# One decoder layer with a mixture of experts on one core: the first slot's turn moved up, and VectorE's last stages moved behind `down`

## The chip, the core and the metric

The kernel runs on one core of a Trainium2 chip. A core has TensorE (PE in the profile, with its weight loads as PEld), VectorE (DVE), ScalarE (ACT), GpSimd (POOL) and SyncE (SP, which here only issues DMAs). Each engine works through its own instructions in the order in which the program issues them, and waits for other engines through semaphores. The metric is the time of one execution on the device in microseconds (us); the profile's span is the stretch inside it from the first to the last recorded event. All times below are of the kernel before.

## The reference: what is computed

The input x has 16 sequences of 128 tokens and 256 channels. Three residual layers follow one another, each on a layer norm of x:

```python
x = x + attn(layernorm(x))       # latent attention: 16 heads, 72 latents, causal
x = x + birwkv(layernorm(x), ctx)
x = x + ffn(layernorm(x))        # 8 experts of 512, two of them for each token

# attn
kv = xn @ latent_w + latent_b;  q[h] = xn @ Wd_w[h] + Wd_b[h]
y[h] = softmax(causal(q[h] @ kv.T / 4)) @ kv;   out = concat(y) @ out_w + out_b
# birwkv: sums over the past and over the future that decay by exp(w) a step, ek = exp(ctx)
wkv = (Af + Ab + exp(u + ctx) * ctx) / (Bf + Bb + exp(u + ctx))
out = sigmoid(xn) * wkv
# ffn: top 2 of 8 by logits, each gate a softmax with far logits masked out
out = sum over the two experts e of gate_e * (silu(xn @ wg[e].T) * (xn @ wu[e].T)) @ wd[e].T
```

All of it is float32.

## The kernel before

**Steps.** The program is one loop over steps s. Steps 0 to 63 are the attention's units: unit s is sequence b = s // 4 and head group s % 4 (four heads each). A unit's scores are computed in step s, its softmax is normalized (`normalize`) in step s + 1, and its probabilities are turned (`turn_probs`: four PE transposes and a copy `aT` by ScalarE) and multiplied with the values in step s + 2. So steps 64 and 65 still hold the end of the attention.

From step 64 on each step also has an expert slot, j = s − 64. A slot is 128 tokens that go to one expert. The loop has 36 of them in its order; three more, which are rarely used, stand behind a condition after slot 27. For slot j:

- `fetch(j)` gathers the 128 rows into `xr` by an indirect DMA that GpSimd issues. It is called three slots ahead.
- `bring(j)` copies the expert's gate weights (ScalarE) and up weights (VectorE) into the buffers `w`. Called one slot ahead.
- `turn(j)` transposes `xr` on PE into the PSUM tile `pxr` and copies that to `xT` (VectorE, L930). Called one slot ahead.
- `up(j)` is two products of 16 matmul records each in the profile: gate product `pg`, then up product `pu` (PE, L966), then `sl` = silu(pg) (ScalarE, L976) and `hT` = sl · pu (VectorE, L978).
- `down(j)` multiplies with the third weight (PE, `pd`, L988), scales by the gate into `y` (VectorE, L999) and adds `y` into the rows of `acc` by an indirect DMA of GpSimd (L1004). Called one slot later: step s holds `up(j)` and then `down(j − 1)`.

**The order inside a step.** Everything else is put into steps by hand. `at(step, place, fn, ...)` notes a piece of work under a step and a place, and `run(s, place)` calls the pieces of that place in the order in which they were noted. As the engines keep the order of issue, the place decides what a piece stands behind on each engine. A slot step of the kernel before issues:

1. `scores` (steps up to 63), `normalize`, place "pre", `turn_probs`, place "A", the maxima and exponentials of the scores (up to 63), place "B", the values' product and its copy out (up to 65);
2. in step 64 only: the attention's pools are closed, the pool `hp` for the slots' tiles is opened, then `bring(0)` and `turn(0)`;
3. `fetch(j + 3)`, `bring(j + 1)`, `up(j)`;
4. place "C";
5. `turn(j + 1)`, `down(j − 1)`.

**What stands in the places around the change.** Each sequence b goes through named stages after its attention; tables (`usual`, `last_but_one` for sequence 14, `last` for sequence 15) give each stage a step, counted from 4b, and a place. In order: `project` (PE, L506, the output projection from the tiles `yP`; the last of nine tiles comes back through DRAM, `rest_values`, L500), `residual` (VectorE: sum and statistics; GpSimd: the reciprocal root `rs_b`, L294), `receptance` (VectorE: two small operations into `nr`, L567, which wait for `rs_b`), `receptance_exp` (ScalarE, exp), `wkv_turn` (PE, `pw`, L584), `mix_1` and `mix_2` (VectorE: L588, a reciprocal L593 and a product L594; then a sum on GpSimd, L595), `mix_stats` (VectorE statistics, GpSimd `rs_c`), `store_sum` (SyncE: the sum to `acc`, L598), `mix_shift` (VectorE: `nb_c`, L314), `mix_row` (ScalarE: the normed row, L611), `store_row` (SyncE, L617), `logits_turn` (PE: two transposes `px`, L626), `logits_turned` (VectorE: copy `x2T`, L631), `logits` (PE: `pl`, L638), `logits_out` (VectorE: `src`, L650).

After every four sequences `route(r)` picks the two experts of 512 tokens. It is a generator; each call does the next part: part 1 and 2 the largest and the second largest logit (VectorE), part 3 the selection and masked gates (VectorE, then an exp on ScalarE), part 4 a running count over tokens on PE (`pf`, L691 to L694) and the gates' sum, part 5 each token's place in the experts' lists and the new totals `taken` (VectorE, L712 to L723). Eight further parts scatter entries into `lists` (GpSimd, L727).

Slots are made from tables: after sequences 7, 11 and 15 a generator (`first_table`, `last_table`) reads the totals through a PE product (`counts`, `pc`, L744) and works out, in some 20 small VectorE operations cut into parts, which expert and which stretch of its list each slot has. `list_slots` then loads the lists' entries (`en`, SyncE, L849).

**PSUM.** Tiles are named by a tag; tag "t" has two buffers that `pt`, `pxr`, `pw` and `px` take in the order of issue, so the third such tile waits until the first has been read. Tag "y" has one buffer for the values' product and, in the first slots, `pu`.

Of the kernel before, what the change touches and what calls it, by code (L numbers as in the profile page):

```python
# [19 lines left out]
B = 16  # L20
T = 128
N = B * T
C = 256
# [49 lines left out]
SLOT0 = NU  # L73
# [6 lines left out]
def decoder_kernel(  # L80
# [30 lines left out]
    st = ctx.enter_context(ExitStack())  # L111
# [316 lines left out]
    def scores(b, hg):  # L428
        g, i = divmod(b, GB)
        ps = bank("s", f"ps_{b}_{hg}").rearrange("p (j t) -> p j t", j=HG)  # L430
        nc.tensor.matmul(ps, identb, maskb, start=True, stop=False)
        for j in range(HG):
            nc.tensor.matmul(  # L433
                ps[:, j, :],
                q[g, hg][0:L, j, ts(i, T)],
                kvT[g][:, ts(i, T)],
                start=False,
                stop=(j == HG - 1),
            )
        pss[b, hg] = ps  # L440
# [466 lines left out]
    hpools, xTs, hTs, regs, useds, brought = [], {}, {}, {}, [], {}  # L907
    experts = {mybir.EngineType.Activation: {}, mybir.EngineType.DVE: {}}

    def bring(j):  # L910


        t, k = slots[j]
        to = []
        for n, (engine, copy) in enumerate(zip(experts, (nc.scalar.copy, nc.vector.tensor_copy))):
            into = experts[engine]
            if k % 4 == 0 or j in RARE:
                load_values(t, "ex", j, k, engine, E - 1, into)
            w = hpools[0].tile([P, WU0], F32, tag=f"w{n}", name=f"w{n}_{j}")
            copy(w, wall[:, bass.ds(into.pop(j), 1), n * WU0 : (n + 1) * WU0].rearrange("p o w -> p (o w)"))  # L920
            to.append(w)
        brought[j] = to

    def turn(j):
        xr = xrs.pop(j)
        pt = bank("t", f"pxr_{j}")
        for c in range(NC):
            nc.tensor.transpose(pt[:, ts(c, P)], xr[:, ts(c, P)], ident)  # L928
        xT = hpools[0].tile([P, NC, P], F32, tag="xT", name=f"xT_{j}")
        nc.vector.tensor_copy(xT, pt[:, : NC * P].rearrange("p (c t) -> p c t", c=NC))  # L930
        xTs[j] = xT
# [49 lines left out]
    def down(j):  # L981
        e = regs.pop(j)
        hT = hTs.pop(j)
        pd = bank("mm", f"pd_{j}")

        def products():
            for f in range(NF):
                nc.tensor.matmul(  # L988
                    pd[:, :C],
                    hT[:, f, :],  # L990
                    wall[:, bass.ds(e, 1), WD0 + f * C : WD0 + (f + 1) * C],
                    start=(f == 0),
                    stop=(f == NF - 1),
                )

        products()
        en = entries.pop(j)
        y = hpools[0].tile([P, C], F32, tag="y", name=f"y_{j}", bufs=3)
        nc.vector.tensor_scalar_mul(y, pd[:, :C], en[:, 2:3].bitcast(F32))  # L999
        if j == SF + S2:  # L1000
            nc.sync.dma_start(out2, acc[0:N, :])

        def add():
            nc.gpsimd.indirect_dma_start(  # L1004
                out=acc if j < SF + S2 else out2,
                out_offset=bass.IndirectOffsetOnAxis(ap=en[:, 1:2], axis=0),
                in_=y,
                in_offset=None,
                compute_op=ALU.add,
            )  # L1010

        add()
# [4 lines left out]
    def at(step, place, fn, *args):  # L1017
        plan.setdefault((step, place), []).append((fn, args))

    def run(step, place):  # L1020
        for fn, args in plan.pop((step, place), []):
            fn(*args)
# [6 lines left out]
    for g in range(1, NG):  # L1029
# [43 lines left out]
    }  # L1073
    last = {
        "residual": (7, "B"),
        "receptance": (7, "C"),
        "receptance_exp": (8, "A"),
        "wkv_turn": (8, "B"),
        "mix_1": (8, "C"),
        "mix_2": (8, "C"),  # L1080
        "mix_stats": (9, "B"),
        "store_sum": (9, "C"),
        "mix_shift": (9, "C"),
        "mix_row": (10, "A"),
        "logits_turn": (10, "B"),
        "logits_turned": (10, "C"),
        "store_row": (10, "C"),
        "logits": (11, "B"),
        "logits_out": (11, "C"),
    }  # L1090
    last_but_one = dict(usual)

# [11 lines left out]
    for name in ("wkv_turn", "mix_1", "mix_2"):  # L1104
        last_but_one[name] = (9, "B")
    for name in ("logits_turn", "logits_turned"):
        last_but_one[name] = (11, "B")
    stages = {
        "residual": residual,
        "receptance": receptance,  # L1110
# [14 lines left out]
    for b in range(B):  # L1125
        s = NHG * b
        if b + 1 < B:
            at(s + 2, "pre", load_ctx, b + 1)
        at(s + 1, "C", wkv_exps, b)
        at(s + 2, "B", wkv_back, b)  # L1130
        at(s + 3, "A", wkv_back_add, b)
        at(s + 4, "B", wkv_forth, b)
        at(s + 5, "A", wkv_forth_add, b)
        at(s + 5, "B", project, b, (0, 1))
        at(s + 6, "B", project, b, (2, 3))
        at(s + 6, "C", rest_values, b)
        at(s + 7, "B", project, b, (4, 5))
        at(s + 7, "C" if b < B - 1 else "B", project, b, (6, 7, NP))
        for name, (step, place) in {B - 2: last_but_one, B - 1: last}.get(b, usual).items():
            at(s + step, place, stages[name], b)  # L1140
        if b < E:
            for k in range(3):
                at(s + 11 + k, "C", load_expert, b, k)
        if b % RB == RB - 1:
            r = b // RB
            parts = ((13, "B"), (13, "C"), (14, "B"), (15, "B"), (15, "C"))
            if b == B - 1:
                parts = ((12, "B"), (12, "C"), (13, "B"), (14, "B"), (14, "C"))
            for step, place in parts:
                at(s + step, place, route_part, r)  # L1150
            for k in range(2 * RB):
                if b < B - 1:
                    at(s + 16 + k, "A", route_part, r)
                else:
                    at(s + 15 + k // 4, "AC"[k // 2 % 2], route_part, r)
        if b + 1 in FIRST_B:
            i = FIRST_B.index(b + 1)
            for k in range(6):
                at(s + 18 + k, "C", table_part, i, first_table, i)
            for k in range(0, S1[i], 2):  # L1160
                at(s + 24 + k // 2, "C", list_slots, min(2, S1[i] - k))
        if b == B - 1:
            for k in range(7):
                at(s + 15 + k // 3, "ABC"[k % 3], table_part, "2", last_table)
            for k in range(0, S2, 4):
                at(s + 17 + k // 4, "C", list_slots, min(4, S2 - k))
            for k in range(4):
                at(s + 20 + k, "B", table_part, "3", very_last)
            for k in range(0, S3, 4):
                at(s + 24 + k // 4, "C", list_slots, min(4, S3 - k))  # L1170
# [41 lines left out]
    for s in range(SLOT0 + len(ORDER) + 1):  # L1212
        j = s - SLOT0
        unit = divmod(s, NHG)
        past = divmod(s - 2, NHG)
        if s < NU:
            scores(*unit)
        if 1 <= s < NU + 1:
            normalize(*divmod(s - 1, NHG))
        run(s, "pre")  # L1220
        if 2 <= s < NU + 2:
            turn_probs(*past)
        run(s, "A")
        if s < NU:
            maxima(*unit)
            exps(*unit)
        g, i = divmod(s, UG)
        tiles = [(0, t) for t in late_tiles.get(s, [])]
        if g + 1 < NG:
            tiles += [(g + 1, t) for t in (TILES_1 if g == 0 else TILES)[i]]  # L1230
        made = [(n, t, *query_tile(n, t)) for n, t in tiles[:2]]
        run(s, "B")
        if 2 <= s < NU + 2:
            values(*past)
            values_out(*past)
        for n, t, pq, to in made:
            query_tile_out(n, t, pq, to)
        for n, t in tiles[2:]:
            query_tile_out(n, t, *query_tile(n, t))
        for n, t in tiles:  # L1240
            if t == NP:
                rest_queries(n)
            if t == 5 and n:
                odd_queries(n, 0)
            if t == 7:
                odd_queries(n, 1)
        if j == 0:

            st.close()
            hpools.append(ctx.enter_context(tc.tile_pool(name="hp", bufs=2)))  # L1250
            bring(0)
            turn(0)
        if j >= 0:
            ahead(j + AHEAD, fetch)
            ahead(j + 1, bring)
            ahead(j, up)
        run(s, "C")
        if j >= 0:
            ahead(j + 1, turn)
            if j >= 1:  # L1260
                down(ORDER[j - 1])
        if j == SF + S2 - SKIP:
            for r in RARE:
                if_used(r, whole_slot)
# [55 lines left out]
```

## Time and profile before

| | us |
|---|---|
| median of 3 runs (567.83, 571.44, 572.62) | 571.44 |
| profiled execution | 571.29 |
| its span | 569.6 |
| PE busy | 523.7 (92%) |
| VectorE busy | 326.8 (57%) |
| ScalarE busy | 293.7 (52%) |
| GpSimd busy | 326.6 (57%) |
| `up(0)` starts (step 64) | 336.09 |
| `up(13)` starts (step 77) | 424.52 |
| last `down` starts | 551.72 |

The span's first 320 us are attention, the stretch from 330 to 424 holds the slots beside the last sequences, routing and tables, and from 424 on there are slots alone. In a timeline row the first two numbers are the start and the duration in us, then engine, line and operation, the tile written and the tiles read, and in brackets how long the engine stood idle before and what released it. In a list of waits the three numbers are the sum in us, how often, and the longest.

### The profile page before, as it was taken

The page shows a single profiled execution, that of the slowest core. Times are in us where ns is not written, and L with a number is a line of the kernel's source. Part 1 is how long each engine was busy: PE and PEld are TensorE (multiplying, and loading weights), DVE is VectorE, ACT ScalarE, POOL GpSimd, SP SyncE. Part 2 cuts the span into 40 slices and gives each one's busy share as a digit, 9 for nine tenths or more (in the row PEclk, how much of TensorE's full clock was granted, in tenths as well). Part 3 has the DMA queues.
Part 4 walks back from the last instruction along what each step waited for, and adds up shares of the span by engine and source line. Part 5 has one row for each costly group of instructions (what it writes and reads, how often), then busy time and mean ns, then how long its engine had stood idle before and what let it go on. Part 6 is the DMA issues. An engine that isn't in the chain of part 4 may idle for free. (4 is left out here: it accounts for less than half of the span.)

```text
span 569.6 us, 10246 instructions
## 1 busy us (share of the span) xinstructions
PE 523.7 (92%) x3317; PEld 447.1 (78%) x3334; DVE 326.8 (57%) x831; ACT 293.7 (52%) x891; POOL 326.6 (57%) x379
## 2 busy tenths in 40 slices
PE   4989999999999999999998959989999999998990
PEld 3767788877877877878876648879989999998990
DVE  3435576577886678878668745555563543433330
ACT  1667776786676777767774744332322323222300
POOL 5355656574787665688636873544486545451532
PEclk9999999999999999999997979999999999999996
DMA  4422145364455544121221111233223333235321
GB/s 144 116 66 74 56 139 181 100 184 126 131 146 152 153 137 150 58 76 40 66 66 44 36 48 30 53 56 57 39 30 50 58 57 47 48 51 171 51 36 18
DMA packets 39662, 47.59 MB, mean 84 GB/s; under 512 B 14136, under 2 KB 31416, under 8 KB 39576
## 3 DMA queue, kind: packets, MB, share of 16 engines
q1 hardware_dynamic: 30106, 37.20, 22.3%
q0 software_dynamic: 7936, 9.51, 10.7%
q8 instruction: 28, 0.46, 0.4%
q10 hardware_dynamic: 1566, 0.21, 0.2%
q14 instruction: 26, 0.21, 0.1%
HBM read 28.22 MB, written 13.31 MB: 73 GB/s over the span
## 5 line engine op out<-in xcount | busy, mean ns | idle before, releaser
L466 POOL TENSOR_TENSOR pr<-pr,rsum 128x512 f32<-128x512 f32 x64 | 76.6, 1197 | 37.2 <-DVE rsum L465 27.8
L453 ACT ACTIVATE pr<-ps,nm 128x128 f32<-128x128 f32 x256 | 90.9, 372 | 10.2 <-DVE nm L445 10.1
L976 ACT ACTIVATE sl<-pg 128x512 f32<-128x512 f32 x36 | 21.5, 598 | 132.4 <-PE pg L966 128.4
L966 PE MATMUL pg<-xT,w 128*128 128x128 f32 x576 | 72.5, 280 | 11.7 <-DVE xT L930 9.8
L966 PEld LDWEIGHTS pg<-xT,w 128*128 128x128 f32 x576 | 70.7, 196 | 15.4 <-issue 14.1
L1004 POOL DMA_INDIRECT acc<-y,en x28 | 47.7, 1705 | 60.9 <-DVE y L999 27.5
L433 PEld LDWEIGHTS ps<-kvT,q 72*128 72x128 f32 x512 | 67.5, 191 | 16.2 <-issue 8.0
L506 PE MATMUL po<-outw_sb,yP 128*128 128x256 f32 x288 | 74.6, 387 | 0.0
L978 DVE TENSOR_TENSOR hT<-sl,pu 128x512 f32<-128x512 f32 x36 | 24.8, 688 | 86.1 <-PE pu L966 80.0
L433 PE MATMUL ps<-kvT,q 72*128 72x128 f32 x512 | 68.8, 276 | 4.3 <-DMA q<-qr 3.1
L966 PE MATMUL pu<-xT,w 128*128 128x128 f32 x576 | 70.5, 276 | 0.0
L988 PE MATMUL pd<-wall,hT 128*128 x288 | 68.0, 379 | 0.0
L966 PEld LDWEIGHTS pu<-xT,w 128*128 128x128 f32 x576 | 67.6, 193 | 0.0
L480 PE MATMUL py<-aT,kvN 128*72 128x512 f32 x128 | 66.6, 602 | 0.3 <-ACT aT L474 0.3
L445 DVE TENSOR_REDUCE nm<-ps 128x4 f32<-128x512 f32 x64 | 43.7, 683 | 37.7 <-PE ps L433 37.7
L398 PE MATMUL pq<-xnT,wq_sb 128*128 128x256 f32 x256 | 64.9, 385 | 0.0
L506 PEld LDWEIGHTS po<-outw_sb,yP 128*128 128x128 f32 x288 | 54.6, 194 | 12.2 <-issue 5.3
L474 ACT COPY aT<-pt 128x512 f32<-128x512 f32 x64 | 37.3, 583 | 44.4 <-PE pt L472 44.1
L988 PEld LDWEIGHTS pd<-wall,hT 128*128 128x128 f32 x288 | 52.0, 190 | 5.6
L453 ACT ACTIVATION_READ_ACCUMULATOR pr<-ps,nm 128x1 f32 x256 | 53.8, 210 | 0.0
L398 PEld LDWEIGHTS pq<-xnT,wq_sb 128*128 128x128 f32 x256 | 45.9, 194 | 4.9 <-issue 0.2
L898 POOL DMA_INDIRECT xr<-xn,en x36 | 37.2, 1034 | 13.4 <-issue 7.4
(171 smaller groups left out, 861.3 us busy)
## 6 DMA issues: line engine op xcount, KB each, us to landing
wall<-in_wg_dram SPq DMA_DIRECT2D x8, 512.0 KB
wall<-in_wu_dram SPq DMA_DIRECT2D x8, 512.0 KB
wall<-in_wd_dram SPq DMA_DIRECT2D x8, 512.0 KB
q<-q SPq DMA_DIRECT2D x16, 224.0 KB
yP<-yB SPq DMA_DIRECT2D x32, 112.0 KB
cx<-in_cx_dram SPq DMA_DIRECT2D x16, 128.0 KB
acc<-x SPq DMA_DIRECT2D x16, 128.0 KB
xn<-row SPq DMA_DIRECT2D x16, 128.0 KB
```

Source lines behind the costliest of these rows:

```text
L398: nc.tensor.matmul(pq[:, :GT], w[:, c, :], xnT[g][:, c, :], start=(c == 0), stop=(c == NC - 1))
L433: nc.tensor.matmul(ps[:, j, :], q[g, hg][0:L, j, ts(i, T)], kvT[g][:, ts(i, T)], start=False, stop=(j == HG - 1),)
L445: nc.vector.tensor_reduce(nm, ps, AX.X, ALU.max, negate=True)
L453: nc.scalar.activation(pr[:, j, :], ps[:, j, :], AF.Exp, bias=nm[:, j : j + 1], accum_out=sums[:, j : j + 1],)
L466: nc.gpsimd.tensor_mul(pr, pr, rsum.unsqueeze(2).to_broadcast([P, HG, T]))
L474: nc.scalar.copy(aT, pt)
L480: nc.tensor.matmul(py[:L], kvN[g][:, ts(i, L)], aTs.pop((b, hg)), start=True, stop=True)
L506: nc.tensor.matmul(pos[b][:, :C], yP[b][:, i, :], outw_sb[:, i, :], start=(i == 0), stop=(i == NP))
L898: nc.gpsimd.indirect_dma_start(out=xr, out_offset=None, in_=xn2[0 : t["rows"], :], in_offset=bass.IndirectOffsetOnAxis(ap=entries[j][:, 0: ...
L966: nc.tensor.matmul(o[:, ts(f, P)], w[:, c * F + f * P : c * F + (f + 1) * P], xT[:, c, :], start=(c == 0), stop=(c == NC - 1),)
L988: nc.tensor.matmul(pd[:, :C], hT[:, f, :], wall[:, bass.ds(e, 1), WD0 + f * C : WD0 + (f + 1) * C], start=(f == 0), stop=(f == NF - 1),)
L1004: nc.gpsimd.indirect_dma_start(out=acc if j < SF + S2 else out2, out_offset=bass.IndirectOffsetOnAxis(ap=en[:, 1:2], axis=0), in_=y, in_of ...
```

## The change

A fourth place "D" is added at the end of a slot step, behind `turn(j + 1)` and `down(j − 1)`. Moved from "C" to "D" are: `receptance`, `mix_1`, `mix_2`, `mix_shift`, `logits_turned` and `logits_out` of sequence 15; `logits_out` of sequence 14; the routing's parts 2 and 5 for the last four sequences; the parts of the second table that fall into steps from 64 on; and two parts of the last table (steps 75 and 76). `logits_turn` and `logits_turned` of sequence 14 go from "B" to "C" of step 67, so from ahead of `up(3)` to behind it. In step 64 `turn(0)`, with the closing of the pools, goes to the head of the step, ahead of `normalize`, and `bring(0)` goes between "A" and "B". No instruction is added or taken away.

```diff
     last = {
         "residual": (7, "B"),
-        "receptance": (7, "C"),
+        "receptance": (7, "D"),
         "receptance_exp": (8, "A"),
         "wkv_turn": (8, "B"),
-        "mix_1": (8, "C"),
-        "mix_2": (8, "C"),
+        "mix_1": (8, "D"),
+        "mix_2": (8, "D"),
         "mix_stats": (9, "B"),
         "store_sum": (9, "C"),
-        "mix_shift": (9, "C"),
+        "mix_shift": (9, "D"),
         "mix_row": (10, "A"),
         "logits_turn": (10, "B"),
-        "logits_turned": (10, "C"),
+        "logits_turned": (10, "D"),
         "store_row": (10, "C"),
         "logits": (11, "B"),
-        "logits_out": (11, "C"),
+        "logits_out": (11, "D"),
     }
...
     for name in ("logits_turn", "logits_turned"):
-        last_but_one[name] = (11, "B")
+        last_but_one[name] = (11, "C")
+    last_but_one["logits_out"] = (12, "D")
...
             if b == B - 1:
-                parts = ((12, "B"), (12, "C"), (13, "B"), (14, "B"), (14, "C"))
+                parts = ((12, "B"), (12, "D"), (13, "B"), (14, "B"), (14, "D"))
...
             for k in range(6):
-                at(s + 18 + k, "C", table_part, i, first_table, i)
+                at(s + 18 + k, "C" if s + 18 + k < SLOT0 else "D", table_part, i, first_table, i)
...
             for k in range(7):
-                at(s + 15 + k // 3, "ABC"[k % 3], table_part, "2", last_table)
+                at(s + 15 + k // 3, "ABD"[k % 3], table_part, "2", last_table)
...
         if s < NU:
             scores(*unit)
+        if j == 0:
+
+            st.close()
+            hpools.append(ctx.enter_context(tc.tile_pool(name="hp", bufs=2)))
+            turn(0)
         if 1 <= s < NU + 1:
             normalize(*divmod(s - 1, NHG))
         run(s, "pre")
         if 2 <= s < NU + 2:
             turn_probs(*past)
         run(s, "A")
+        if j == 0:
+            bring(0)
...
-        if j == 0:
-
-            st.close()
-            hpools.append(ctx.enter_context(tc.tile_pool(name="hp", bufs=2)))
-            bring(0)
-            turn(0)
         if j >= 0:
             ahead(j + AHEAD, fetch)
             ahead(j + 1, bring)
...
             if j >= 1:
                 down(ORDER[j - 1])
+        run(s, "D")
```

## The prediction

> **What bounds it now.** I read the busy shares first, then TensorE's waits, then the timeline from the last attention step to slot 13, then the chain that ended last. PE is busy 92% of the span, so only its idle stretches and what runs behind its end can give time.
>
> ```profile
> PE 523.7 (92%) x3317; PEld 447.1 (78%) x3334; DVE 326.8 (57%) x831; ACT 293.7 (52%) x891; POOL 326.6 (57%) x379
> ...
> 529.81 0.22 PE pxr L928 x2
> 530.02 1.73 PE pd L988 x8
> 531.75 1.78 PE pg L966 x16
> 533.54 1.79 PE pu L966 x16
> ```
>
> The first line is the profile's summary. The last four lines are one slot in the chain that ended last: 0.22 + 1.73 + 1.78 + 1.79 = 5.52 us, PE without a gap. So a gain or loss of PE in slots 0 to 13 travels to the end unchanged: behind PE stand only y (555.37), the scatters and the rest, each started by what PE finished. Which waits does PE have there?
>
> ```profile
> PE pg L966 <- DVE xT L930: 9.8, 4, 6.3
> ...
> PE px L626 <- ACT row L611: 1.3, 1, 1.3
> ...
> PE pw L584 <- DVE xT L930: 0.7, 1, 0.7
> ...
> 333.54 0.15 DVE L567 TENSOR_SCALAR nr<-rs_b 128x1 f32<-128x1 f32 x1 [2.41 <-POOL rs_b L294]
> 335.53 0.41 DVE L930 COPY xT<-pxr 128x256 f32<-128x256 f32 x1
> 336.09 3.75 PE L966 MATMUL pg<-xT,w 128*128 128x128 f32 x16 [6.26 <-DVE xT L930]
> 339.63 2.25 PE L966 MATMUL pu<-xT,w 128*128 128x128 f32 x16
> ...
> 374.94 0.42 DVE L594 TENSOR_TENSOR r<-pw,r 128x256 f32<-128x256 f32 x1
> 375.29 0.41 DVE L930 COPY xT<-pxr 128x256 f32<-128x256 f32 x1
> 375.84 2.02 PE L966 MATMUL pg<-xT,w 128*128 128x128 f32 x16 [2.08 <-DVE xT L930]
> ```
>
> The first lines say that PE's `up` waits for the copy xT, four times. The second group is the worst: slot 0's xT stands in VectorE's queue behind `receptance` (nr), which waits for GpSimd. Also see that pg takes 3.75 us and pu 2.25 after this 6.26 us gap, not 1.95 each; the granted clock was 0.50 from 334 to 338. The third group is step 69: xT behind mix_2's multiply, 2.08 us; behind it pg takes 2.02, at clock 1.00.
>
> **A ruler for a slot step.** Let T be the start of `up` (pg). From the steady slot at 526.07: hT starts at T+3.84, xT of the next slot at T+4.45, ending T+4.87; PE is free for the next `up` at T+5.52; y starts at T+5.72, and VectorE is free again at T+6.12. xT to pg takes 0.14 (375.70 to 375.84), so xT has 0.5 us to spare. In the next step (T' = T+5.52) VectorE is free from T'+0.60 and hT is due at T'+3.84; the copy w takes 0.6, so places D and B together have 2.6 us, 3.1 with the spare.
>
> **Part 1, slot 0 (step 64).** New order: pxr before turn_probs, xT before normalize. xr_0 was issued at 324.48 and landed 3.2 us later, so pxr runs at 327.75. VectorE leaves the table's L820 at 329.46; xT ends at 329.88. px now reuses the PSUM buffer of pxr, so it waits for xT: 330.02. It takes 0.25, the values product 0.86: `up(0)` at **331.15** instead of 336.09. ScalarE's copy w, no longer behind the values' copy, ends near 330.4; VectorE's follows residual at 331.2 to 331.9, pu needs it at 332.9. With no long gap pg and pu take 3.58 together, not 5.65 (336.09 to the logits at 341.72). The next limit is unmoved: rs_b on GpSimd gives nr at 333.54, then the scan (1.21), w (0.6), and hT starts at 335.55 instead of pu's 335.0; xT_1 ends 336.6, pw (waits for that PSUM buffer) starts 336.7; projection and values follow, and `up(1)` starts at 338.9, before 345.90: 7.0 us.
>
> One cost is unshown. VectorE's w copy now falls beside GpSimd's gather at 330.96 and its normalize. Nearest row: the gather at 335.08, which ran beside such copies, took 1.58 us, the median 1.00. So between 0 and 0.6; I take 0.6, since it is the same pair of operations, and rs_b then holds hT: **6.4**. The Trainium skill, "SBUF — State Buffer" (Who interferes with whom), says that a copy of this kind and a GpSimd operation exclude each other for their whole length; by it the sum is this one, without it 0.6 us better.
>
> **Part 2, transposes of sequence 14 behind `up(3)`.** px waited 1.3 us for row; from pd's end to px 1.5 us were lost. Behind `up` row has been ready for 3 us. Gain 1.5, here 7.9. What is late next: the projection's last tile needs the store at L500, which SyncE issues behind acc's store, which waits for scatter 0: 7.0 us after pd(0) starts (356.72 − 349.69), about 2.0 to land (a weight load at 287.97 waited for one issued at 285.94). The tile's turn comes at 9.8 (pd 1.73, projection 0.86, a slot 5.52, eight matmuls 1.72), so 0.8 is left and I charge nothing; GpSimd being later by one lists scatter (1.3) would cost 0.5.
>
> **Part 3, receptance and mix of sequence 15.** Step 68: nr(15) now follows y(2) and six table operations (0.7), so ScalarE's exp ends 1.4 after `up(4)`, its w at 2.4, table load to 3.65, sl 4.25; hT is 0.45 late, xT 0.45, within the spare. `up(5)` comes without its wait: in before, step 68 took 7.76, now 5.52. Gain 2.2, here **10.1**.
>
> **What it costs: hand-offs.** D stands behind y, and y behind pd. Where PE's next step opens with a product of what D made, PE now waits:
> - Step 69 to 70. D of 68 (src, mix_1, reciprocal, multiply) ends at T'+3.3, GpSimd's sum at 4.2, statistics and w at 5.8: hT is 2.0 late (4.5 us of work against 2.6). xT ends at T'+6.85, y takes 0.4, nb 0.15, row 0.60; px, first in step 70, starts at T'+8.05 instead of 5.52. Loss 2.5, less 0.1 of step 69 before: 2.4, here 7.7.
> - Step 71: px's copy follows y (T+6.12), 0.42, plus 0.14: logits at 6.68 instead of 5.52. Loss 1.15, here 6.5.
> - Step 73: part two of routing no longer holds xT (0.33, and 0.2 in step 72): gain 0.5. ScalarE's exp is 0.9 later, then w and table load: xT_10 0.25 late. Here 6.8.
> - Step 75: the counts need `taken`:
>
> ```profile
> 411.42 0.17 DVE L723 TENSOR_TENSOR taken<-taken,new 128x8 f32<-128x8 f32 x1
> 411.50 0.42 DVE L930 COPY xT<-pxr 128x256 f32<-128x256 f32 x1
> 411.73 0.36 PE L744 MATMUL pc<-taken,ones 128*128 128x8 f32 x2 [0.19 <-DVE taken L723]
> ```
>
> `taken` stood ahead of xT. Now: y, then 410.30 to 411.59 again (1.29), 0.14: T+7.55, before T+5.96. Loss 1.6, here 5.2.
> - Step 76: the table's ten operations (1.8) leave xT's path: PE's 1.11 wait and 0.2 go, gain 1.4. But D of 75 (1.9), then 76's two parts (0.6, 1.4) and the register load (0.4) make 4.3 us: hT 1.4 late, xT_13 ends T'+6.3, `up(13)` 0.9 late. Here 6.6, then **5.7**.
>
> Steps 65, 66, 74, 77 and later carry under 2.6 us and cost nothing. The moved parts hold no DMA of SyncE; GpSimd's list scatters need `place`, 1.7 later against VectorE, but they stand behind add(9) (412.58 to 414.18) anyway. Slot 17's gather landed about 439.5 for a use at 444.72: 5 us of cover.
>
> **Sum.** 6.4 + 1.5 + 2.2 − 2.4 − 1.15 + 0.25 − 1.6 + 1.4 − 0.9 = 5.7 us. The profiled execution took 571.29 (span 569.6 and 1.7 around it): **565.6**. The median of the runs, 571.44, is the same within 0.03%. This is 1.0%, the size that a measurement of this kernel can just tell from no change.
>
> **Rivals.**
> - *Hand-offs are dearer* (569.0): each of px, logits, counts and xT_13 costs 0.8 more than my chain of rows, through later semaphores or GpSimd beside VectorE; the store at L500 belongs here. For: small VectorE operations are stretched now and then beside GpSimd's (L820 1.71, L314 0.99 for 0.15). Against: from 380 on, when GpSimd does scatters and gathers, L820 took 0.15. Chance 0.18.
> - *D costs nothing* (559.6): the losses of 2.4, 1.15, 1.6 and 0.9, 6.0 in all, stay away as PE finds other work. Half of them would give 562.6. Against: PE's queue is in order, and row, logits and counts head their steps. Chance 0.12.
> - *The clock shuts in the new waits* (slower, 574.0): after 6.26 us without work pg and pu lost 2.1 us; after 2.08 nothing. px15 waits 2.5, the counts 2.0. If waits from 2 us on counted, or four waits within 25 us added up, four times 2.1 is 8.4: 571.3 − 5.7 + 8.4. It decides if a wait of 2.5 us halves the clock. Against: 2.08 at step 69 and 1.92 at 514.96 left pg at 2.02. With the head's two waits of about 1 us each (ahead of pxr and of px) counted too it is 578. Chance 0.10, half of it for each. The Trainium skill, "TensorE: Matmul & The Clock Gate" (What's actually happening), puts the idle window at about 3.4 us; both rows agree with it, and by it this rival fails.
>
> **Numbers.** Forecast 0.60, 562.5 to 568.5 by its bounds: the 0.6, L500's 0.5, 0.4 for each of four hand-offs, and 1 us for the head, where xr_0 or L820 may shift. It lies on the edge of 1% (565.6 against 565.7), so half of it, 0.31, counts as faster; with the 0.12 of the free case that is 0.43. Slower by over 1% is 0.05, from the clock; the rest, 0.52, is within 1%. The range, 560.0 to 571.0, leaves out the clock and the best half of the free case.
>
> **What would show it.** Right: `up`'s wait for xT at slot 0 gone and pg(0) near 1.95; px of sequence 14 without wait; new waits of PE for row (about 2.5), the copy x2T (1.2), `taken` (2) and xT in step 77 (0.9). Wrong: a gather of xr_0 that lands after 329, a pu(0) waiting for w, PE waiting for L500's store, clock under 1.00 between 365 and 420, or a wait for xr_17.

## The result, and the profile after

The changed kernel takes 568.08 us (median; 562.97 to 569.64), the kernel before 570.37. The ratio is 0.9948, 95% interval 0.9930 to 0.9967: about 3.0 us faster (1.9 to 4.0), inside 1%; the medians are 2.3 us apart. The ratios leave out executions in a slow state, of which only e1_head below has any, three of its twelve, at 576.01 to 577.00 us. Forecast were 565.6 us and a gain of 5.7, so the time lies in the range (560.0 to 571.0), and the gain is about half of what was forecast. The profiled execution took 567.05 us with a span of 565.4.

The summary of the page of the changed kernel, with the row of the granted clock:

```profile
span 565.4 us, 10244 instructions
...
PE 525.5 (93%) x3317; PEld 448.8 (79%) x3334; DVE 330.1 (58%) x831; ACT 293.4 (52%) x891; POOL 326.1 (58%) x379
...
PEclk9899999999999999999997989989999999999996
```

PE does the same work as before and is busy 1.8 us longer (525.5 against 523.7): a busy time that grows with no instruction added is the first sign of a lower clock. In the row of the clock, a digit for each 14.1 us, the stretches 325 to 339 us and 368 to 382 stand at 8, and one at the start, 14 to 28; the kernel before has a 7 at the first, slot 0's gap, and nothing at the two others. The 7 ahead of them (297 to 311) stands in both.

TensorE's waits in the changed kernel (sum in us, how often, the longest):

```profile
PE px L626 <- ACT row L611: 2.1, 1, 2.1
...
PE pc L744 <- DVE taken L723: 1.8, 1, 1.8
PE px L626 <- DVE rsum L465: 1.4, 1, 1.4
...
PE pg L966 <- DVE xT L930: 1.0, 2, 0.8
PE pxr L928 <- DMA xr<-xn,en: 0.9, 1, 0.9
PE pl L638 <- DVE x2T L631: 0.9, 1, 0.9
```

The 9.8 us for xT have become 1.0. In their place stand the hand-offs that were forecast: row 2.1 (forecast 2.5), `taken` 1.8 (2.0), x2T 0.9 (1.15), xT in step 77 0.8 (0.9). The two waits of step 64, 0.9 ahead of pxr and 1.4 ahead of px, were forecast as about 1 us each. As a list of waits the prediction came true. What was not in its sum is behind the waits, on the timeline of the changed kernel:

```profile
329.48 0.66 PE L626 MATMUL px<-ident,row 128*128 128x128 f32 x2 [1.41 <-DVE rsum L465]
329.93 1.91 PE L480 MATMUL py<-aT,kvN 128*72 128x512 f32 x2
331.24 1.77 DVE L920 COPY w<-wall 128x1024 f32 x1 [0.65 <-DVE mvb L292]
331.64 2.47 PE L966 MATMUL pg<-xT,w 128*128 128x128 f32 x16
333.95 1.95 PE L966 MATMUL pu<-xT,w 128*128 128x128 f32 x16
...
372.60 0.60 ACT L611 ACTIVATE row<-x,nb_c,rs_c 128x256 f32<-128x256 f32 x1 [4.51 <-DVE nb_c L314]
373.25 0.44 PE L626 MATMUL px<-ident,row 128*128 128x128 f32 x2 [2.13 <-ACT row L611]
373.53 3.48 PE L966 MATMUL pg<-xT,w 128*128 128x128 f32 x16
376.80 2.10 PE L966 MATMUL pu<-xT,w 128*128 128x128 f32 x16
...
407.76 0.39 PE L744 MATMUL pc<-taken,ones 128*128 128x8 f32 x2 [1.76 <-DVE taken L723]
408.00 2.03 PE L966 MATMUL pg<-xT,w 128*128 128x128 f32 x16
```

Slot 0 starts at 331.64 and not at 336.09, but the values' product py takes 1.91 us (in the steady steps before it 1.08) and pg 2.47 instead of 1.95. Behind the wait of 2.13 us for row, pg takes 3.48: 1.53 lost, and 0.15 more on pu. Behind the wait of 1.76 us for `taken`, pg takes 2.03: nothing lost. The stretches of the same execution (start:end and length, then the busy time of PE, its weight loads, VectorE, ScalarE and GpSimd, then the granted clock, the DMA share and GB/s):

```profile
330.00:332.00 2.00, 2.00 (x5) 0.87 (x4) 1.29 (x4) 0.12 (x1) 1.67 (x3) 0.50 0.23 66
...
370.00:374.00 4.00, 1.87 (x11) 1.40 (x10) 3.27 (x9) 1.40 (x2) 2.91 (x3) 0.96 0.23 64
374.00:376.00 2.00, 2.00 (x12) 2.00 (x11) 0.00 (x0) 0.14 (x1) 1.70 (x2) 0.50 0.64 110
376.00:378.00 2.00, 2.00 (x15) 2.00 (x15) 0.00 (x0) 0.90 (x2) 0.10 (x1) 0.73 0.49 104
```

The clock is 0.50 from 330 to 332 and from 374 to 376: it falls after the wait, while the matmuls run, and not in the wait itself. So there is a lead for the missing 2 to 3 us. It is also in the spread: of the 22 executions the six at a mean clock of 0.984 to 0.986 took 562.97 to 565.24 us, the other sixteen, at 0.971 to 0.979, took 567.0 to 569.6.

### The profile page after: what moved, and what is told of

It reads as the page before. It is cut to its first block, busy times and chain, and to the rows that moved or that the text cites. A ratio compares the mean times of both kernels' runs of the same rounds, so it can differ in the third digit from the quotient of the medians.

```text
span 565.4 us, 10244 instructions
## 1 busy us (share of the span) xinstructions
PE 525.5 (93%) x3317; PEld 448.8 (79%) x3334; DVE 330.1 (58%) x831; ACT 293.4 (52%) x891; POOL 326.1 (58%) x379
```

## The experiments

Two theories were put against each other: that the hand-offs cost what the sum says and the clock what is missing, and that the moved parts themselves are dearer than the sum. No kernel here leaves out any of the computation; fillers, where there are any, write to a PSUM tile that nothing reads. Diffs are against the changed kernel unless the text says otherwise. The kernels ran in three groups on three chips: e1 to e4; after_again, e5_warm, e6 and e7; e5_again, e8, e9 and e10. Within a group all share the runs of the kernel before.

### The head alone, and the places alone

`e1_head` is the kernel before with nothing but the head of step 64 moved, `e2_places` the changed kernel with that move undone.

```diff
 # e1_head, against the kernel before; e2_places is the reverse, against the changed kernel
+        if j == 0:
+            st.close()
+            hpools.append(...)
+            turn(0)
         if 1 <= s < NU + 1:
             normalize(*divmod(s - 1, NHG))
...
         run(s, "A")
+        if j == 0:
+            bring(0)
...
-        if j == 0:
-            st.close(); hpools.append(...); bring(0); turn(0)
```

> Only the move of the first slot's turn and bring; all places as before. Theory (the head gives most, the places net lose): up(1) starts about 6.1 us earlier against the step before it, as in the kernel after, pg(0) near 1.95 to 2.5 us, then the old waits for row of sequence 14 (1.3), for xT at step 69 (2.1) and step 76 (1.1) are back; time 6 us under the kernel before, about 564.5, so faster than the kernel after (568.1). Rival (the places give the gain, the head's wait is only moved): 1 us under before or less, about 569.5. Rival (both parts help a little): about 569.

> Only the places (D and the transposes of sequence 14 behind up(3)); slot 0's turn where it was. Theory: slot 0 keeps its wait of about 6.3 us; the places lose more at row, x2T, taken and xT of step 77 than they gain at row of sequence 14, at step 69 and at step 76: 2.2 us slower than before by the differences of starts from up(1) to up(13) in the two traces, about 572.5, with a granted clock of 0.5 somewhere from 373 us on. Rival (the places help): 1 to 3 us faster than before, 567.5 to 569.5.

Measured: e1_head has a ratio of 0.9901 (0.9865 to 0.9938), 5.7 us faster; by all twelve executions it is less, 4.1 us by the means and 3.1 by the medians (572.35 against 575.46). e2_places 575.96, ratio 1.0016 (0.9985 to 1.0047), 0.9 us slower, between 0.9 faster and 2.7 slower. So **the gain is the head's** (term: 6.4), and no gain of the places together is shown (their terms add up to −0.7). The traces agree on the head: counted from the same product py of the attention (324.45 before, 321.07 in e1_head), `up(1)` starts 6.0 us sooner. The theory of the clock had expected e2_places to lose 2.2 us; the interval leaves that open.

TensorE's instructions in slot 0 of e1_head:

```profile
326.63 0.41 PE L626 MATMUL px<-ident,row 128*128 128x128 f32 x2 [1.24 <-DVE took L820]
327.73 1.95 PE L966 MATMUL pg<-xT,w 128*128 128x128 f32 x16
330.31 2.02 PE L966 MATMUL pu<-xT,w 128*128 128x128 f32 x16 [0.63 <-DVE w L920]
...
366.48 2.02 PE L966 MATMUL pg<-xT,w 128*128 128x128 f32 x16 [2.09 <-DVE xT L930]
```

The same order of work as in the changed kernel, with the same short wait ahead of px, but here pg takes 1.95 us. And the wait of 2.09 for xT at step 69, which this kernel has kept, is followed by a pg at full speed, as it was in the kernel before (2.08, then 2.02). In the trace of e2_places the other kind of wait shows:

```profile
377.15 0.44 PE L626 MATMUL px<-ident,row 128*128 128x128 f32 x2 [2.13 <-ACT row L611]
377.42 2.66 PE L966 MATMUL pg<-xT,w 128*128 128x128 f32 x16
379.88 2.90 PE L966 MATMUL pu<-xT,w 128*128 128x128 f32 x16
```

Here 0.71 and 0.95 us are lost, 1.66 in all, behind a wait for row as long as the harmless one for xT. Neither the length of a wait nor its place in the program says alone whether the clock falls; what does is worked out with the fillers below.

### Which places to leave out, and which parts to put later

`e3_pick` keeps the head, sequence 14 and the tables, and takes back each hand-off that the sum charged: sequence 15's mix and logits, and part 5 of the routing. `e4_late` keeps all the moves, and moves the consumers too, behind `up`, the last table's parts later.

```diff
 # e3_pick
-        "receptance": (7, "D"),   "mix_1": (8, "D"),  "mix_2": (8, "D"),
-        "mix_shift": (9, "D"),    "logits_turned": (10, "D"),
+        "receptance": (7, "C"),   "mix_1": (8, "C"),  "mix_2": (8, "C"),
+        "mix_shift": (9, "C"),    "logits_turned": (10, "C"),
-                parts = ((12, "B"), (12, "D"), (13, "B"), (14, "B"), (14, "D"))
+                parts = ((12, "B"), (12, "D"), (13, "B"), (14, "B"), (14, "C"))
 # e4_late
-        "logits_turn": (10, "B"),  "logits": (11, "B"),
+        "logits_turn": (10, "C"),  "logits": (11, "C"),
-            for k in range(7):
-                at(s + 15 + k // 3, "ABD"[k % 3], table_part, "2", last_table)
+            for step, place in ((15, "D"), (16, "A"), (16, "D"), (17, "A"), (17, "D"), (18, "A"), (18, "A")):
+                at(s + step, place, table_part, "2", last_table)
-                at(s + 17 + k // 4, "C", list_slots, min(4, S2 - k))
+                at(s + 18 + k // 4, "B", list_slots, min(4, S2 - k))
```

> The kernel after with the places of receptance, mix_1, mix_2, mix_shift, logits_turned (sequence 15) and routing's part 5 put back to C; the head, the transposes of sequence 14, routing's part 2 and the tables stay as in the kernel after. Theory (hand-offs to PE's next step cost the difference): PE's waits for row of sequence 15 (2.1), x2T (0.9) and taken (1.8) go, xT's wait of 2.1 at step 69 comes back, no halved clock behind row; gain over before 6.1 + 1.8 + 0.2 + 0.5 = 8 to 9 us, about 562. Rival (the difference lies in DVE's load, wherever the parts stand): within 1 us of the kernel after, 567 to 569.

> The kernel after with the consumers moved instead: logits_turn and logits of sequence 15 from B to C (behind up(6) and up(7)), and the parts of the last table one or two places later each, with counts behind down(10) and the lists loaded one step later. Theory (hand-offs): PE's waits for row, x2T and taken are gone with all of D kept; xT of step 70 is still late by about 1.4 us (D of 68 and B of 69 make 4.5 us of VectorE's work); gain over before about 10 us, 559 to 561. Rival (VectorE's load): as the kernel after, 567 to 569. Rival (the later lists make slot 17 wait): a wait for its gather at step 80 and no gain.

Measured: e3_pick 566.13 us, ratio 0.9841 (0.9796 to 0.9886), 9.2 us faster than the kernel before; e4_late 565.15, ratio 0.9806 (0.9770 to 0.9842), 11.2 faster. Both agree with the hand-offs being real losses of the change: taking them back, or giving their consumers time, is worth several us. e4_late lost its waits for `taken` and x2T as meant (pc at 409.14 without a wait), but a wait of 1.14 for hT in front of `up(6)` shows the limit of place "D": the mix of step 68 holds up hT, and with it xT, of step 69.

These two traces also show something that no theory held. VectorE in e3_pick, and in e4_late:

```profile
418.95 0.60 ACT L976 ACTIVATE sl<-pg 128x512 f32<-128x512 f32 x1 [7.26 <-PE pu L966]
...
422.68 0.69 DVE L978 TENSOR_TENSOR hT<-sl,pu 128x512 f32<-128x512 f32 x1 [5.58 <-remote]
```

```profile
418.05 0.69 DVE L978 TENSOR_TENSOR hT<-sl,pu 128x512 f32<-128x512 f32 x1 [4.88 <-remote]
```

At steps 76 to 77 VectorE stands idle for 5.58 and 4.88 us ahead of hT, and for the last 3.1 and 3.8 us of it both inputs are there: in e3_pick ScalarE ended sl at 419.55 (418.95 + 0.60) and PE pu at 418.83. ScalarE is late as well: sl starts about 2 us later against pu than in the other slots (0.2 us after pu's start). "remote" means that the trace has no releaser for it. PE then waits 3.07 and 4.17 us, with pg at 3.53 and 3.54. e1_head, where PE waits 2.40 us at the same place, has hT 2.7 us after the end of pu, and e2_places has its hT at 432.51, 2.8 us after the end of pu. In the traces from other chips nothing is released by "remote" there. It may be part of why the kernel before took 575.46 on this chip against 570 elsewhere; there is no trace of before from this chip to tell. I leave the cause open, and take the sizes of this group's gains, that of e4_late above all, with reserve until its parts ran elsewhere (below).

### The clock by itself

Next the waits were filled with work, to hold the clock and leave the order of everything else. `e5_warm` gives PE identity products in two of the waits: six ahead of px of sequence 13 (step 64), nine ahead of px of sequence 15 (step 70), all ahead of the wait for the input. `e8_turnfill` is the same with transposes in place of products, to ask whether these count as work for the clock: the short head waits have transposes between them, and the clock fell there. `e5_again` is e5_warm a second time.

```diff
 # in logits_turn, ahead of the two transposes px
+        for k in range({B - 3: 6, B - 1: 9}.get(b, 0)):
+            if k == 0:
+                fill = bank("s", f"fill_{b}")
+            nc.tensor.matmul(fill[:, ts(k % 4, P)], ident, ident, start=True, stop=True)
 # e8_turnfill: the last line is
+            nc.tensor.transpose(fill[:, ts(k % 4, P)], ident, ident)
```

> The kernel after, unchanged, beside the others on one chip. Theory: ratio to before 0.993 to 0.9967 as measured first. Rival (the result hangs on the chip): outside of that.

> The kernel after with filler products of the identity on TensorE (their result is not used) ahead of px of sequence 13 in step 64 (6, about 1.3 us) and ahead of px of sequence 15 in step 70 (9, about 2.0 us): they fill the waits of 1.4 and 2.1 us there. Theory (the granted clock is halved after these waits): py stays near 1.08 us and pg(0) and pg(6) near 1.95 (1.91, 2.47 and 3.48 in the kernel after), the granted clock is 1.00 there, and the time is 2 to 3 us under that of the kernel after. Rival (the clock does not hang on these waits): the same low clock, the same time within 0.5 us.

> As e5_warm, but the filler in the two waits is of transposes of the identity, the same number and place. Theory (the clock counts transposes little or not: a wait of 2.1 us with px behind it cost the clock, one of 2.1 us ahead of pg at step 69 did not): the low clock and the long pg come back, ratio to before 0.994 to 0.997 as for the kernel after. Rival (any work of TensorE keeps the clock): as e5_warm, near 0.9905.

> e5_warm unchanged, to stand beside e8_turnfill on one chip: 0.988 to 0.993 of before.

| kernel | median, us | before, us | ratio (95%) |
|---|---|---|---|
| after_again | 567.98 | 570.21 | 0.9962 (0.9940 to 0.9983) |
| e5_warm | 564.85 | 570.21 | 0.9905 (0.9884 to 0.9926) |
| e5_again | 565.12 | 571.48 | 0.9895 (0.9860 to 0.9929) |
| e8_turnfill | 565.32 | 571.48 | 0.9898 (0.9868 to 0.9928) |

With work for PE in the two waits the change gains 5.4, 6.4 and 6.2 us by the medians, and without it 2.2 in the same group as e5_warm; the intervals of after_again and e5_warm do not meet. So **filling the two waits, which holds the clock there, gives about 3.1 us, and with it the gain is near the forecast 5.7.** The traces account for 2.3 of the 3.1: 1.68 behind row and 0.6 on the way to `up(1)`. The rest is inside the intervals; losses behind the wait for `taken`, which e5_warm doesn't fill, may be in it. The changed kernel shows the same without a filler: its six executions at a clock of 0.984 to 0.986 (562.97 to 565.24 us) took what those of e5_warm took, at 0.984 to 0.987 (563.33 to 565.45).

The trace of after_again has three losses: at slot 0 (pg 2.80), behind row, and behind the wait for `taken`, which cost nothing in the first trace of the same kernel:

```profile
374.93 0.44 PE L626 MATMUL px<-ident,row 128*128 128x128 f32 x2 [2.14 <-ACT row L611]
375.20 3.17 PE L966 MATMUL pg<-xT,w 128*128 128x128 f32 x16
378.16 2.41 PE L966 MATMUL pu<-xT,w 128*128 128x128 f32 x16
...
409.44 0.39 PE L744 MATMUL pc<-taken,ones 128*128 128x8 f32 x2 [1.77 <-DVE taken L723]
409.69 3.64 PE L966 MATMUL pg<-xT,w 128*128 128x128 f32 x16
```

Behind `taken` it is 1.77 us of waiting, then 3.64 instead of 1.95. In e5_warm the same place at row is:

```profile
369.38 2.17 PE L627 MATMUL fill<-ident 128*128 128x128 f32 x18
371.68 0.44 PE L630 MATMUL px<-ident,row 128*128 128x128 f32 x2
371.95 1.95 PE L970 MATMUL pg<-xT,w 128*128 128x128 f32 x16
```

The filler takes the place of the wait: px comes when row is there, and pg is at 1.95 with the clock at 1.00. In e8_turnfill:

```profile
371.64 1.15 PE L627 MATMUL fill<-ident 128*128 128x128 f32 x9
373.93 0.44 PE L630 MATMUL px<-ident,row 128*128 128x128 f32 x2 [1.15 <-ACT row L611]
374.20 1.95 PE L970 MATMUL pg<-xT,w 128*128 128x128 f32 x16
```

Nine transposes take half the time of nine products (the records count two for each product), so 1.15 of the wait are left, and still pg is at 1.95. My theory that transposes don't count for the clock **fell**: they cut the stretch without work as products do.

**When a wait strikes.** The granted clock in the traces changes only at the ends of windows of 3.41 us. Up to 540 us every stretch at half clock, in all fourteen traces, lasts 3.41 or 6.83 us, and the stretches at full clock between them are whole multiples of 3.41. Against the span the windows lie elsewhere in each execution. With them known, the busy time of TensorE can be read for each:

| trace, wait (us) | window or windows that hold it, us | PE busy in it, us | clock of the next window |
|---|---|---|---|
| changed kernel, row (2.13) | 370.27 to 373.68 | 1.28 | 0.50 |
| after_again, row (2.14) | 372.29 to 375.70 | 1.27 | 0.50 |
| e2_places, row (2.13) | 375.05 to 378.46 | 1.31 | 0.50 |
| e10_before_warm (below), xT at step 69 (2.09) | 370.68 to 374.09 | 1.32 | 0.50 |
| before, xT at step 69 (2.08) | 370.98 to 374.39, and the next | 2.78 and 1.96 | 1.00 |
| e6_mix (below), xT at step 69 (2.02) | 364.25 to 367.66, and the next | 1.80 and 3.02 | 1.00 |
| e1_head, xT at step 69 (2.09) | 362.83 to 366.24, and the next | 1.56 and 3.18 | 1.00 |
| after_again, `taken` (1.77) | 406.42 to 409.83 | 1.64 | 0.50 |
| changed kernel, `taken` (1.76) | 404.40 to 407.81 | 1.65 | 1.00 |
| changed kernel, step 64 (0.93 and 1.41) | 325.90 to 329.31 | 1.24 | 0.50 |
| e1_head, step 64 (1.10 and 1.24) | 321.87 to 325.28, and the next | 2.31 and 2.17 | 1.00 |

A wait of 2 us that lies in one window leaves too little work in it, and the whole next window runs at half clock; the same wait divided over two windows costs nothing. From 320 to 540 us the fourteen traces have 882 windows at full clock. Half clock followed on all 17 with PE busy for less than 1.56 us, on two of the five between 1.56 and 1.65, and on none of the other 860. So the same program loses the clock in one execution and not in the next. The busy time is not quite what the clock goes by: near 299 us, in the attention, half clock followed on 1.90 to 2.25 us in thirteen of the fourteen traces.

### The receptance and mix taken back

`e6_mix` puts `receptance`, `mix_1`, `mix_2` and `mix_shift` back to "C", and leaves the rest of the change. It asks what part 3 is worth with the clock in it.

```diff
-        "receptance": (7, "D"),  "mix_1": (8, "D"),  "mix_2": (8, "D"),  "mix_shift": (9, "D"),
+        "receptance": (7, "C"),  "mix_1": (8, "C"),  "mix_2": (8, "C"),  "mix_shift": (9, "C"),
```

> The kernel after with receptance, mix_1, mix_2 and mix_shift of sequence 15 back in C; everything else as in the kernel after. Theory (moving the mix trades a wait of 2.1 us for one of 2.1 us, and the later one costs the clock): xT's wait of 2.1 at step 69 is back, row's wait at step 70 is gone, the clock stays at 1.00 behind step 70: 1.5 to 2 us under the kernel after. Rival (no clock cost): equal to the kernel after within 0.4 us. Rival (the mix in D is a gain by itself): 2 us over the kernel after.

Measured: 565.32 us, ratio 0.9912 (0.9890 to 0.9935), 2.7 us less than after_again. More than the 1.5 to 2 expected, but with after_again's interval (±1.2) it agrees. In its trace the old wait is back, and the new one is gone with its clock:

```profile
368.06 2.02 PE L966 MATMUL pg<-xT,w 128*128 128x128 f32 x16 [2.02 <-DVE xT L930]
...
373.66 0.38 PE L626 MATMUL px<-ident,row 128*128 128x128 f32 x2
373.88 1.95 PE L966 MATMUL pg<-xT,w 128*128 128x128 f32 x16
```

So part 3 of the change, as a whole, made the kernel slower: it traded a wait of 2 us for one as long, and the new one had the clock behind it in both traces of the changed kernel.

### Filling a wait in the kernel before

If 2.1 us are lost to the clock behind slot 0's wait in the kernel before, filling that wait alone should give them. `e10_before_warm` is the kernel before with 24 identity products in slot 0's `turn`.

```diff
 # against the kernel before, in turn(j)
+        if j == 0:
+            fill = bank("s", "fill")
+            for k in range(24):
+                nc.tensor.matmul(fill[:, ts(k % 4, P)], ident, ident, start=True, stop=True)
```

> The kernel before with 24 filler products (about 5.4 us) on TensorE in slot 0's wait of 6.3 us, behind pxr. Theory (of the 5.65 us of pg(0) and pu(0) 2.1 are the halved clock): the wait ends where it did, pg(0) takes 2.0 and pu(0) 1.95, the time falls by 2 us (0.9965 of before). So some 2 us of what the head's move gives are clock. Rival (the filler delays up(0), or the clock stays low): no change or slower.

Measured: 571.66 against 571.48 us, ratio 0.9992 (0.9960 to 1.0024). The 2 us did not come; the interval just holds the expected 0.9965. Its trace shows one place where they can go:

```profile
335.27 2.02 PE L970 MATMUL pg<-xT,w 128*128 128x128 f32 x16 [0.91 <-DVE xT L934]
...
373.05 2.81 PE L970 MATMUL pg<-xT,w 128*128 128x128 f32 x16 [2.09 <-DVE xT L934]
375.65 2.83 PE L970 MATMUL pu<-xT,w 128*128 128x128 f32 x16
```

pg of slot 0 is at 2.02, as meant. But the wait for xT at step 69, 2.09 us, which left the clock alone in before, e1_head and e6_mix, is now followed by 2.81 and 2.83: 1.7 us lost. One trace shows that this can happen, not that it happens in most executions; but the twelve fall into two groups, four at a clock of 0.988 (566.25 to 569.10 us) and eight at 0.978 to 0.982 (570.83 to 573.23), as with a loss that comes and goes. Whether the filler moves this wait against the clock's windows is not shown.

### Moving the consumers too

`e7_all` is e4_late with sequence 15's statistics, shift and row put later, into place "D" of step 69 and "B" and "C" of step 70, so that nothing between "D" and the next `up` is in a hurry. `e9_best` adds six filler products in step 64, and puts the transposes of row and the store of row into "D" of step 70.

```diff
 # e7_all, on top of e4_late
-        "mix_stats": (9, "B"),  "mix_shift": (9, "D"),   "mix_row": (10, "A"),
+        "mix_stats": (9, "D"),  "mix_shift": (10, "B"),  "mix_row": (10, "C"),
 # e9_best, on top of e7_all, with the six products of e5_warm ahead of px of sequence 13
-        "logits_turn": (10, "C"),  "store_row": (10, "C"),
+        "logits_turn": (10, "D"),  "store_row": (10, "D"),
```

> e4_late with the statistics of sequence 15 moved on: mix_stats from B of step 69 to D, mix_shift to B of 70, mix_row to C of 70 ahead of logits_turn. Theory (a step's D and following B may hold 2.6 us of VectorE's work): hT(5) is on time, up(6) comes without its wait of 1.1 us; 1 us under e4_late, 11 to 12 us under before. Rival (row now comes late for logits_turn behind up(6)): a wait for row at step 70 and no gain.

> e7_all with the filler products ahead of px of sequence 13 in step 64 (6), and with logits_turn and store_row of sequence 15 in D of step 70, behind down(5). Theory: py near 1.08 and pg(0) near 2.0 (1.74 and 2.93 in e7_all), no wait for row (0.9 there): 2 us under e7_all's ratio of 0.981, so 0.977 to 0.979 of before. Rival (the clock falls again elsewhere): as e7_all.

Measured: e7_all 559.48 us, ratio 0.9809 (0.9785 to 0.9833), 10.9 faster than before and 8.5 faster than the change. e9_best **557.74**, ratio 0.9769 (0.9735 to 0.9802), 13 us faster than before. TensorE in e9_best:

```profile
327.93 1.50 PE L627 MATMUL fill<-ident 128*128 128x128 f32 x12
329.41 0.41 PE L630 MATMUL px<-ident,row 128*128 128x128 f32 x2
329.65 1.02 PE L480 MATMUL py<-aT,kvN 128*72 128x512 f32 x2
330.51 1.95 PE L970 MATMUL pg<-xT,w 128*128 128x128 f32 x16
...
359.32 1.95 PE L970 MATMUL pg<-xT,w 128*128 128x128 f32 x16
...
364.84 1.95 PE L970 MATMUL pg<-xT,w 128*128 128x128 f32 x16
...
370.36 1.95 PE L970 MATMUL pg<-xT,w 128*128 128x128 f32 x16
```

`up(4)`, `up(5)` and `up(6)` are 5.52 us apart, the distance of the steady slots: nothing waits between them. That bears the account out from the other side. The limits of 5.52 us a slot and of what "D" may hold were right, and the hand-offs were the loss; e7_all on a chip without VectorE's stall also bears out what e4_late gave.

## Why the prediction was right and where it was wrong

The table goes by the prediction's own steps. A term is the change in the distance between two starts of `up`, before against after, in the profiled executions. The attention ahead ran 0.54 us quicker in the second execution, which is no work of the change and is taken off the first term.

| step | forecast, us | measured, us |
|---|---|---|
| head, to `up(1)` | 6.4 | 6.60 − 0.54 = 6.06 |
| px of sequence 14 behind `up(3)` | 1.5 | 1.76 − 0.21 = 1.55 |
| no wait for xT at step 69 | 2.2 | 2.24 |
| px of sequence 15 waits for row | −2.4 | −2.27 |
| logits wait for x2T (step 71) | −1.15 | −2.80 |
| steps 72 to 74 | 0.25 | 0.00 + 0.49 − 0.28 = 0.21 |
| counts wait for `taken` | −1.6 | −1.47 |
| step 76 without its wait | 1.4 | 1.26 |
| xT of slot 13 late | −0.9 | −0.90 |
| sum to `up(13)` | 5.7 | 3.88 |

Eight of nine terms are within 0.35 us, so the bound (PE's order), the 5.52 us a slot, the 2.6 us that places D and B may hold, and the hand-offs were read rightly from the rows before. What they show together is also in the experiments: the head alone gives 4 to 6 us, the places alone nothing.

**The step that failed** is the one that priced the wait of px for row as a wait alone and left its clock out. Of the −2.80 at step 71, 1.53 is pg at 3.48 and 0.15 is pu at 2.10: the clock of 0.50 behind that wait. The remaining 1.1 is x2T, as forecast. The prediction had this as a rival, with the right place and mechanism: it "decides if a wait of 2.5 us halves the clock". It gave it 0.10 and priced it at 2.1 for each of four waits. It was half true: the loss falls behind the wait of 2.1 for row in all three traces that have it (changed kernel twice, e2_places), behind `taken` in two of seven traces with that wait (after_again, e2_places; pg at 2.03 in the others). Each time pg and pu together lose nearly the same: 1.68, 1.68 and 1.66 behind row, 1.76 and 1.75 behind `taken`. So the price of one loss is 1.7 us, not 2.1, however long the wait was (1.77 to 2.14): one window of 3.41 us at half clock. What varies is whether it strikes, and that goes by where the wait lies against the clock's windows, which neither the forecast nor the rival had. In the medians the two filled waits are worth 3.1 us, between the forecast (0) and the rival (8.4). My evidence against it, two rows with waits of 2.08 and 1.92 us and no loss, was too thin: it was one execution, in which both waits happened to be divided over two windows (PE busy 2.78 and 1.96 us, and 2.13 and 2.78). The like wait at step 69 (2.01 to 2.09 us) cost nothing in four traces (before, e1_head, e3_pick, e6_mix) and 1.74 us in a fifth (e10_before_warm).

The Trainium skill, "TensorE: Matmul & The Clock Gate" (What's actually happening), puts the idle window at about 3.4 us, and I let that settle the rival. The runs do not bear that use out: a clock of 0.50 came after 2.13, 2.14, 1.77 and 2.09 us without work, in part of the executions. The same section calls the window free-running, with an effect that differs from run to run, and gives about 3.4 us of work at half clock until it rises. The traces agree with that: their windows are 3.41 us, they lie elsewhere in each execution, and a loss is 1.7 us; but a window need not be idle from end to end, 1.24 to 1.32 us of work in it did not hold the clock.

**The head** came 0.3 us under its term. The price for VectorE's copy beside GpSimd was right in kind: w took 1.77 us and not 0.69, close to 0.69 and the 1.05 of GpSimd's normalize (331.40 to 332.45) one after the other, and rs_b ended at 333.45, so nr came at 333.48 and, with the 0.54 us that all was early, 0.48 later than in the kernel before. The prediction charged 0.6. The head's clock (py 1.91, pg 2.47) made `up(0)` late by 1.0 us against the forecast 331.15, but about half of it is hidden: hT waits for nr and the copy anyway. In e5_warm, where the clock held, the head gives 6.6 by the same count, 0.2 over its term; so the near match of 6.06 is luck in part. It also hides a sign that the prediction had named as one of being wrong, pu(0) waiting for w: where the clock held, that wait is there, 0.63 us in e1_head, e5_again, e8_turnfill and e9_best.

**The two other rivals.** "D costs nothing" fell: row, `taken` and x2T were waited for. "Hand-offs are dearer" fell too, as to hand-offs: the four waits are each within 0.4 of forecast, and all below it. The total that it gave, 569.0 (its own terms add up to 568.8), is near the 568.08 for another reason. The store at L500 was never waited for.

## What to carry to other kernels

When a producer is moved behind the long operations of an in-order engine, move its consumer as far on too: the change moved only producers and gained 2 to 3 us, with consumers moved as well it was 11 to 13. Price each wait of TensorE from about 1.8 us on (3.41 less 1.65), or shorter ones that add up to that within 3.4 us, with the clock behind it: a loss of 1.7 us that strikes where one window of the clock happens to hold the whole wait, so in part of the executions. Don't exclude it on one trace; read the busy time window by window, and take two traces of the same kernel. Where such a wait can't be moved, a few identity products ahead of it, from data that are there, held the clock here.

## What the runs showed of the hardware that was not expected

- The clock fell to 0.50 after waits of 1.77 to 2.14 us, in some executions and not in others, with the same program: pg behind `taken` took 2.03 in one execution of the changed kernel and 3.64 in another. The clock changes at the ends of windows of 3.41 us, which lie elsewhere in each execution; between 320 and 540 us it halved after each window with TensorE busy for less than 1.56 us, and after none with more than 1.65. What it measures exactly stays open: near 299 us, 1.90 us were not enough.
- Step 64 of the changed kernel lost clock after waits of 0.9 and 1.4 us with only a few transposes between them (py 1.91 for 1.08, pg 2.47), as both lay in one window (1.24 us busy); e1_head with 1.10 and 1.24 did not, as they lay in two (2.31 and 2.17). Transposes as filler held the clock as well as products did (0.9898 and 0.9895).
- On one chip VectorE stood idle for 2.7 to 3.8 us at step 76 or 77 with both inputs of hT ready, in two of the four traces with no releaser; in those two ScalarE was late as well. The four kernels, with more or fewer of the moves, all had it, and no trace from the other chips had it: there an hT for which VectorE is idle starts 0.1 us after its later input. Its cause was not found.
